# Turning the normed tokens in 32x32 blocks on VectorE and placing the blocks by transfers through DRAM, instead of transposing them on TensorE

## The chip, the cores and the metric

The kernel runs on one core of a Trainium2 chip. The metric is the device time of one execution in microseconds. The kernel was timed three times before the change; the median counts. TensorE (PE) multiplies matrices and transposes by a matmul with the identity, VectorE (DVE) and ScalarE (ACT) work on elements, GpSimd (POOL) does a little of the same, and SyncE (SP) issues nearly all transfers. Each engine works through its own instructions in order and waits on semaphores for the others.

## The reference

Four layers are chained on `x`, 8 sequences of 256 tokens of 512 features, all float32. Three of them contain a step "normalize every token, scale and shift its features by a vector that belongs to the sequence, multiply by weights"; it is this step that the change touches, five times over: the attention and the MLP of layer 0, the attention and the MLP of layer 1, and the attention of layer 2. Layer 3 (eight small experts with a norm) is not touched.

```python
# layer 0 (ada_rms, twice: ahead of the attention and of the MLP)
n = x * jax.lax.rsqrt(jnp.mean(jnp.square(x), axis=-1, keepdims=True) + EPS)
scale = t @ tw.T
return n * (w * (1.0 + scale))[:, None, :]
...
q = (h @ Wq.T).reshape(b, s, NQ, HD).transpose(0, 2, 1, 3)
scores = jnp.einsum('bkgsd,bktd->bkgst', qg, k) / jnp.sqrt(jnp.float32(HD))
attn = jax.nn.softmax(scores, axis=-1)
x = res + ctx @ Wo.T
...
mlp = jax.nn.silu(h @ Wg.T) * (h @ Wu.T) @ Wd.T
```

Layer 1 has a norm with mean and variance, 16 heads of 32 and a GELU MLP; layer 2 the same norm, 16 heads on 4 key heads, and a mask.

## The kernel before

A sequence is two tiles of 128 tokens by 512 features (tokens on the partitions). All products need the features on the partitions, so every normed sequence is transposed to `hT` (128 x 4 x 256: four chunks of 128 features by 256 tokens).

`normed` (L414) takes mean and variance by bn_stats and bn_aggr (L422, L423) on DVE, the power -1/2 on POOL (L430, L431), and writes the normed tile to a buffer `n` (L436 for layer 0's form, L438 for the other), once for each of the two tiles. `h` (L479) is a generator: it calls `normed`, pauses, and lets `feature_major` (L464) transpose chunk by chunk on TensorE (L471, eight 128x128 transposes for a sequence, into two PSUM banks `C`). Each chunk is evicted from PSUM with its scale and shift by `modulated` (L456): DVE for the first two chunks (L450 in layer 0, L460 in layers 1 and 2), ACT for the other two (L454, L462). `h` is called 40 times: 8 sequences in each of the five steps.

Work that isn't on the main line is a list of generators, `queue`. The main line calls `some(us)` (L196), which gives them a credit of microseconds of TensorE time; each `yield` says how much was used, and `yield None` ends a turn. `rest` (L210) drains the queue. On top of this a scheduler reorders the finished program on each engine, so that instructions can stand earlier than the code's order.

`attend` (L536) is the main line of the three attentions. A step handles one sequence b and one group g of four heads: `scored` (L569, TensorE into four PSUM banks `A`), `softmax` (L575: the row maxima on DVE, L583 or, with a bias, L591; the exponentials on ACT, L596; the reciprocal of the sums L602, its turn in 32x32 blocks L606, a store of 16 KB to DRAM L609, and loads that broadcast the rows over the partitions, L614: two of 128 KB in attention 0, one in attentions 1 and 2). One step later the group's probabilities are transposed (`turned`, L626, with evictions by `copy`, L448 on DVE and L452 on ACT), multiplied by the values (`weighted`, L641) and scaled by the broadcast inverses (`ctxT`, L653). Attention 0 has two groups per sequence, attentions 1 and 2 four. At g == 0 the queue is drained, and `project(b + 1)` is put into it: `h` of the next sequence, the products of its queries, keys and values (`product_steps`, L512), the rotary terms or norms (L530, L531, L1246 to L1258), and the transposes of queries and keys (L1019, L1234). The output projection with `wo` (L512) and the sum into `x` (L1075, L1210) follow when all groups are done. `work` holds the TensorE time that a sequence's share of the queue takes.

`mlp` (L777) walks over 64 steps: two halves hh of the inner features, 8 sequences, four steps p each. A step has the products of `begun` and `ended` (L793), sums on ACT and DVE (L811 to L814, L823), and the products of `lower` (L842). In the first half, at p == 0, the queue gets `following(b + 1)` (L869): `h` of the next sequence, the sums that `blocked` (L750) forms of its chunks, and their stores to DRAM (L755, L757), from which the second half loads them again (L763, L766). In the second half's last sequence the next attention's `project(0)` is in the queue.

SP issues the transfers of weights (L734, L745), the `spread` stores and loads, and those of `blocked`, in one queue. `hT` has two buffers.

Of the kernel before, what the change touches and what calls it, by code (L numbers as in the profile page):

```python
# [20 lines left out]
F32 = mybir.dt.float32  # L24
# [6 lines left out]
P = 128  # L31
B, S, D = 8, 256, 512
NT = B * S // P
TB = S // P
KC = D // P
# [133 lines left out]
class Program:  # L169
    def __init__(self, ctx, tc, d, out):  # L170
        self.ctx, self.tc, self.nc, self.d, self.out = ctx, tc, tc.nc, d, out
        self.n = 0
        self.queue, self.credit = [], 0.0

    def pool(self, name, psum=False):
        return self.ctx.enter_context(
# [19 lines left out]
    def some(self, us):  # L196


        self.credit += us
        while self.credit > 0 and self.queue:  # L200
            try:
                did = next(self.queue[0])
            except StopIteration:
                self.queue.pop(0)
                continue
            if did is not None:
                self.credit -= did
            elif us < 1e6:
                break

    def rest(self):
        self.some(1e9)
        self.credit = 0.0

# [2 lines left out]
    def setup(self):  # L217
        nc, d = self.nc, self.d
        self.const = self.pool("const")
        self.xp = self.pool("xp")  # L220
        self.wqkvp = self.pool("wqkvp")
        self.wop = self.pool("wop")
        self.wbigp = self.pool("wbigp")
        self.work = self.pool("work")
        self.psum = self.pool("psum", psum=True)

        def c(shape, tag, **kw):
            return self.t(shape, tag, pool=self.const, **kw)

        self.condT = c([P, KC, 32], "condT")  # L230
        nc.gpsimd.memset(self.condT, 0.0)
        nc.sync.dma_start(
            self.condT[:, :, :B], d["condT"].rearrange("(k p) b -> p k b", p=P)
        )
        self.x = [self.t([P, D], f"x{i}", pool=self.xp) for i in range(NT)]
        self.tw = self.columns("tw1T", 1)
        for i in range(TB):
            self.load_x(i)
        self.vec = c([P, N_VEC], "vec")
        nc.sync.dma_start(self.vec, d["vec"])  # L240
        self.pos = c([P, NT], "pos", dtype=I32)
        nc.sync.dma_start(self.pos, d["posT"])
        self.inv_freq = c([P, 32], "inv_freq")
        nc.sync.dma_start(self.inv_freq, d["inv_freq"].to_broadcast([P, 32]))

        self.ident = c([P, P], "ident")
        make_identity(nc, self.ident)
        self.neg_half = c([P, 32], "neg_half")
        nc.gpsimd.memset(self.neg_half, -0.5)
        self.inv = [c([P, 32], f"inv{i}") for i in range(2)]  # L250
        for t in self.inv:
            nc.gpsimd.memset(t, 0.0)
        self.spread = [
            self.tc.dram_tile([32, P], F32, name=f"spread{i}") for i in range(4)
        ]
        self.n_spread = 0
        self.half_pi = c([P, 1], "half_pi")
        nc.gpsimd.memset(self.half_pi, math.pi / 2)

        self.mod0 = c([P, 8, B], "mod0")  # L260
        self.mod1 = c([P, 16, B], "mod1")
        self.mod2 = c([P, 8, B], "mod2")
        self.mod3 = c([P, 8, B], "mod3")
        self.scondT = c([P, KC, 32], "scondT")
        nc.scalar.activation(self.scondT, self.condT, AF.Silu)
# [145 lines left out]

    def normed(self, xs, eps, rms=False):  # L414

        nc = self.nc
        n = len(xs)
        mv = self.t([P, n, 2], f"mv{n}", 2)
        r = self.t([P, n], f"r{n}", 2)
        for i, x in enumerate(xs):  # L420
            st = self.t([P, 6], "st", 3)
            nc.vector.bn_stats(st, x)  # L422
            nc.vector.bn_aggr(mv[:, i, :], st)  # L423
        mean, var = mv[:, :, 0], mv[:, :, 1]
        if rms:
            nc.vector.tensor_tensor(r, mean, mean, ALU.mult)
            nc.vector.tensor_tensor(r, r, var, ALU.add)
            nc.gpsimd.tensor_scalar(r, r, eps, None, ALU.add)
        else:
            nc.gpsimd.tensor_scalar(r, var, eps, None, ALU.add)  # L430
        nc.gpsimd.tensor_tensor(r, r, self.neg_half[:, 0:n], ALU.pow)  # L431
        rows = []
        for i, x in enumerate(xs):
            y = self.bank("n")
            if rms:
                nc.vector.tensor_scalar(y, x, r[:, i : i + 1], None, ALU.mult)  # L436
            else:
                nc.vector.tensor_scalar(  # L438
                    y, x, mv[:, i, 0:1], r[:, i : i + 1], ALU.subtract, ALU.mult
                )  # L440
            rows.append(y)
        return rows
# [33 lines left out]
            evacuate(c0, m.rearrange("p (c t) -> p c t", c=2))  # L476
            yield 0.87

    def h(self, b, eps, mod, scale_at, shift_at, rms=False, blocks=False):  # L479


        rows = self.normed([self.x[TB * b + t] for t in range(TB)], eps, rms)
        yield None
        hT = self.t([P, KC, S], "hT")

        def place(c):
            if not blocks:
# [1 line left out]
            at = 2 * (c // 2)  # L489
            return hT[:, at : at + 2, P * (c % 2) : P * (c % 2 + 1)]  # L490

        def evacuate(c0, m):
            for c in range(2):
                scale = mod[:, scale_at + c0 + c, b : b + 1]
                shift = None if shift_at is None else mod[:, shift_at + c0 + c, b : b + 1]
                in_ = m[:, c, :]
                if blocks:
                    in_ = in_.rearrange("p (t q) -> p t q", t=TB)
                self.modulated(c0 // 2, place(c0 + c), in_, scale, shift)

        yield from self.feature_major(rows, evacuate)
        yield None
        return hT

    def product(self, *args):
# [27 lines left out]

    def attend(self, n_groups, hd, project, value, finish, work, key_tiles=(2, 2), biased=None,  # L536
               extra=None, then=None, spare=None, inverse=None):

# [11 lines left out]
        nc = self.nc  # L552
# [3 lines left out]
        at = [0, wide[0]]  # L556
# [104 lines left out]
        for i in range(B * n_groups + 1):  # L661
# [19 lines left out]
                    turned(j, last[2][0][j])  # L681
            if ahead is not None:
                ahead = (b, g, softmax(ahead[2]))
            if last is None:
                self.some(3 * quantum)
            else:
# [79 lines left out]
            self.nc.sync.dma_start(t, kept[b, :, (4 + i) * S : (5 + i) * S])  # L766
        return hT, ts

    def mlp_input(self, *args, **kw):

        self.hT = yield from self.h(*args, **kw)

    def mlp_begin(self, name):
        self.kept = self.tc.dram_tile([B, P, 7 * S], F32, name=name)
# [252 lines left out]

    def project0(self, b, got):
        nc, w, cos, sin = self.nc, self.w0, self.cos, self.sin
        hT = yield from self.h(b, 1e-6, self.mod0, 0, None, rms=True)  # L1030
        qT = self.t([P, KC, S], "qT")
        kT, v = self.keys_values(b, ((S,), (TB, 64)))
        turn = []
# [43 lines left out]
    def layer0_attention(self):  # L1077
        self.ups = []

        def conditions(b):  # L1080
# [6 lines left out]
            else:  # L1087
# [4 lines left out]
                    self.layer0_up(i if i >= 0 else -1 - i, int(i >= 0))  # L1092

        self.attend(
            2, 64, self.project0, lambda v, g, j, k: v[:, k, :],
            lambda b, ctxT: self.added(b, ctxT, self.w0o), (10.5, 6.8),
            extra={
                0: (conditions(0), 7.7), 2: (conditions(2), 4.6),
                5: (self.sums_of_ups(0, 2), 0.0), 6: (self.sums_of_ups(2, 4), 0.0),
                7: (self.mlp_input(0, 1e-6, self.mod0, 4, None, rms=True, blocks=True), 1.74),  # L1100
            },
            then=lambda: self.mlp_begin("kept0"),
            spare=lambda: [self.ups[i][1][:, 7, :] for i in range(4)],
            inverse=[self.w0[:, k, 640:896] for k in range(4)],
        )

    def layer0_up(self, i, which):
# [8 lines left out]
    def layer0_mlp(self):  # L1116
# [52 lines left out]
        def finish(hh, b, ys):  # L1169
# [3 lines left out]

        self.mlp(
            ups, downs, down_sums, lambda i: self.layer0_up(4 + i, 1), load_next, act,
            lambda b: self.h(b, 1e-6, self.mod0, 4, None, rms=True, blocks=True), finish,
            (self.project1(0, self.got), 23.0),
        )


# [33 lines left out]
    def project1(self, b, got):  # L1214
# [2 lines left out]
        def heads(t):  # L1217
            return t.rearrange("p (h e) -> p h e", e=32)

        hT = yield from self.h(b, 1e-6, self.mod1, 0, 8)  # L1220

        def part(t, i):
            m = self.bank("C")
# [66 lines left out]
    def layer1_attention(self):  # L1290
# [32 lines left out]
        def value(v, g, j, k):  # L1323
            return v[:, k, (4 * g + j) * 32 : (4 * g + j + 1) * 32]

        self.attend(
            4, 32, self.project1, value, finish, (23.0, 6.8), biased=self.bias,
            extra={
                4: (self.sums_of_ups(0, 2), 0.0), 5: (self.sums_of_ups(2, 4), 0.0),
                7: (self.mlp_input(0, 1e-6, self.mod1, 4, 12, blocks=True), 1.74),  # L1330
            },
            then=lambda: self.mlp_begin("kept1"),
            spare=lambda: [self.ups[i][0][:, 7, :] for i in range(4)],
            inverse=[self.downs[i][2] for i in range(4)],
        )

    def layer1_up(self, i):
# [9 lines left out]
    def layer1_mlp(self):  # L1347
# [22 lines left out]
        def finish(hh, b, ys):  # L1370
# [8 lines left out]
        self.mlp(  # L1379
            self.ups, self.downs, lambda i: self.rights(*self.downs[i][0], *self.downs[i][1]),  # L1380
            lambda i: self.layer1_up(4 + i), lambda i: self.layer1_down(4 + i), act,
            lambda b: self.h(b, 1e-6, self.mod1, 4, 12, blocks=True), finish,
            (self.project2(0, self.got), 11.3),
        )


# [15 lines left out]

    def project2(self, b, got):
        nc, w = self.nc, self.w2
        hT = yield from self.h(b, 1e-5, self.mod2, 0, 4)
        qT = self.t([P, KC, S], "qT")
        kT, v = self.keys_values(b, ((S,), (TB, P)))
        m = self.bank("C")[:, :S]
# [32 lines left out]
    def layer2(self):  # L1441
        self.load_layer3()
        spare = self.t([P, 8, S], "wbig")
        self.attend(
            4, 32, self.project2, lambda v, g, j, k: v[:, k, j * 32 : (j + 1) * 32],
            lambda b, ctxT: self.added(b, ctxT, self.w2o), (11.3, 6.8), key_tiles=(1, 2),
            biased=self.mask, extra={7: (self.expert_inputs(0), 1.74)},
            spare=lambda: [spare[:, i, :] for i in range(4)],
            inverse=[spare[:, i, :] for i in range(4, 8)],
# [180 lines left out]
```

## Time and profile before

| | us |
|---|---|
| median of three timed runs | 2167.53 |
| lowest and highest | 2165.76, 2169.83 |
| profiled execution, its time | 2161.66 |
| its span, first to last instruction | 2159.9 |
| attention 0 with the setup | to about 280 |
| MLP 0 | 280 to 876 |
| attention 1 | 876 to 1310 |
| MLP 1 | 1310 to 1705 |
| attention 2 | 1705 to 2010 |
| experts (layer 3) | 2010 to 2159 |

The granted TensorE clock was 0.992 on average. The rows by line that concern the transposed tokens (line, engine, operation, tile, shape, count; then total busy time and mean ns of one; then idle time before and what ended it):

| line | engine | what | count | mean ns |
|---|---|---|---|---|
| L471 | PE | transpose of a 128x128 block of `n` | 320 | 290 |
| L436, L438 | DVE | normed tile, 128x512 | 32, 48 | 593, 644 |
| L450, L460 | DVE | chunk of `hT` from PSUM, 128x256 | 32, 48 | 475, 535 |
| L454, L462 | ACT | chunk of `hT` from PSUM, 128x256 | 32, 48 | 488, 557 |
| L606 | DVE | turn in 32x32 blocks, 128x32 | 80 | 206 |

Busy time of pipelined matmuls overlaps, so eight transposes cost less than eight times their mean. The transfers moved 106.71 MB in 93,425 packets, 49 GB/s over the span.

### The profile page before, as it was taken

The numbers are of one execution on the slowest core, as the hardware profiler recorded it, in microseconds if no ns is written. First come the engines' busy times: TensorE is split into PE (matmuls) and PEld (weight loads), VectorE is DVE, ScalarE is ACT, GpSimd is POOL, SyncE is SP. The second block draws the span as 40 slices with busy tenths as digits, with TensorE's granted clock in tenths as the row PEclk, the third lists the DMA queues.
The fourth block names the chain that finished last, engine by engine and source line by source line (L and its number), as shares of the span: only waits on it lengthen the run. The fifth ranks groups of instructions, "written<-read, shape, count | busy, mean of one in ns | idle before, by whom it ended". The sixth has DMA issues, their size and how long they took to land.

```text
span 2159.9 us, 36437 instructions
## 1 busy us (share of the span) xinstructions
PE 2089.9 (97%) x13522; PEld 1550.8 (72%) x13522; DVE 1335.2 (62%) x4444; ACT 757.2 (35%) x2330; POOL 293.5 (14%) x308
## 2 busy tenths in 40 slices
PE   7999999999999999999999999999999989999999
PEld 4555679999999999765555557999999855554444
DVE  6866665655666555665556566666666577676333
ACT  3423421111111111155555552222222255555644
POOL 2111100000000000334444341000000001010220
PEclk9999999999999999999999999999999999999999
DMA  8310230000320100210000022113211100000001
GB/s 303 115 56 21 69 124 18 30 24 18 90 78 21 33 18 18 69 44 19 17 20 17 12 63 68 45 62 93 93 48 45 49 20 18 18 19 20 6 35 44
DMA packets 93425, 106.71 MB, mean 49 GB/s; under 512 B 16512, under 2 KB 67392, under 8 KB 93248
## 3 DMA queue, kind: packets, MB, share of 16 engines
q1 hardware_dynamic: 93248, 104.38, 15.0%
q8 instruction: 107, 1.75, 0.3%
q14 instruction: 70, 0.57, 0.1%
HBM read 84.14 MB, written 20.22 MB: 48 GB/s over the span
## 4 chain that ended last, share of the span: by engine, by line
PE 86%; DVE 7%; DMA 3%; ACT 2%; POOL 1%; issue 1%; SPq 0%; ACTq 0%; DVEq 0%; POOLq 0%
PE C L793 28%; PE C L512 23%; PE A L842 18%; PE C L626 5%; PE A L569 4%; PE C L641 3%; DMA wqkv<-spread 1%; PE A L1499 1%; DVE p L591 1%; ACT p L596 1%; PE C L471 1%; PE C L1517 1%; DVE n L438 1%; DVE p L448 1%; DVE st L422 1%
## 5 line engine op out<-in xcount | busy, mean ns | idle before, releaser
L793 PE MATMUL C<-hT,wbig 128*128 128x128 f32 x3072 | 416.1, 275 | 2.6 <-DVE p L814 2.6
L793 PEld LDWEIGHTS C<-hT,wbig 128*128 128x128 f32 x3072 | 388.6, 192 | 11.8 <-issue 5.2
L793 PE MATMUL C<-ctxT,wbig 128*128 128x128 f32 x2304 | 319.8, 275 | 0.0
L512 PE MATMUL C<-wqkv,hT 128*128 128x512 f32 (+1 forms) x768 | 311.7, 545 | 4.0 <-DVE p L448 3.3
L596 ACT ACTIVATE p<-p,low 128x256 f32<-128x256 f32 (+1 forms) x512 | 241.1, 472 | 204.3 <-DVE low L591 202.9
L793 PEld LDWEIGHTS C<-ctxT,wbig 128*128 128x128 f32 x2304 | 288.0, 192 | 0.0
L842 PE MATMUL A<-wbig,p 128*128 128x256 f32 x1024 | 242.5, 379 | 0.0
L591 DVE CUSTOM_DVE_ANT_0 p<-A,row 128x256 f32<-128x256 f32 (+1 forms) x512 | 171.3, 386 | 90.3 <-PE C L641 65.9
L512 PEld LDWEIGHTS C<-wqkv,hT 128*128 128x128 f32 x768 | 129.9, 191 | 120.9 <-issue 110.8
L842 PEld LDWEIGHTS A<-wbig,p 128*128 128x128 f32 x1024 | 189.5, 190 | 23.1
L823 DVE TENSOR_TENSOR p<-p,C 128x256 f32<-128x256 f32 x192 | 79.1, 418 | 168.9 <-PE C L793 166.8
L811 ACT COPY p<-C 128x128 f32<-128x128 f32 x192 | 50.9, 265 | 376.8 <-PE C L793 376.8
L626 PEld LDWEIGHTS C<-ident,p 128*128 128x128 f32 x1152 | 130.6, 143 | 68.9 <-issue 40.7
L626 PE MATMUL C<-ident,p 128*128 128x128 f32 x1152 | 162.8, 282 | 9.7 <-ACT p L596 5.3
L512 PE MATMUL C<-wo,ctxT 128*128 128x512 f32 x336 | 158.4, 611 | 6.7 <-DVE ctxT L653 6.6
L430 POOL TENSOR_SCALAR r<-mv 128x2 f32<-128x2 f32 (+1 forms) x28 | 6.4, 230 | 865.7 <-DVE mv L423 865.2
L812 DVE TENSOR_TENSOR p<-p,C 128x128 f32<-128x128 f32 x192 | 54.5, 284 | 109.3 <-ACT p L811 107.4
L1156 ACT ACTIVATE p<-C 128x128 f32<-128x128 f32 x64 | 17.7, 277 | 285.4 <-DVE p L823 285.4
L512 PEld LDWEIGHTS C<-wo,ctxT 128*128 128x128 f32 x336 | 60.8, 193 | 79.2 <-issue 60.4
L448 DVE COPY p<-C 128x512 f32<-128x512 f32 (+1 forms) x160 | 100.6, 630 | 26.4 <-PE C L626 25.7
L596 ACT ACTIVATE p<-A,low 128x256 f32<-128x256 f32 x128 | 59.3, 477 | 120.5 <-DVE low L583 88.3
L452 ACT COPY p<-C 128x512 f32<-128x512 f32 (+1 forms) x160 | 85.1, 532 | 33.1 <-PE C L626 32.9
(214 smaller groups left out, 3054.4 us busy)
## 6 DMA issues: line engine op xcount, KB each, us to landing
kept<-hT SPq DMA_DIRECT2D x16, 512.0 KB
hT<-kept SPq DMA_DIRECT2D x16, 512.0 KB
wbig<-spread SPq DMA_DIRECT2D x64, 128.0 KB
wbig<-in_wada1T SPq DMA_DIRECT2D x6, 1024.0 KB
kept<-ctxT SPq DMA_DIRECT2D x48, 128.0 KB
ctxT<-kept SPq DMA_DIRECT2D x48, 128.0 KB
n<-gammas SPq DMA_DIRECT2D x24, 256.0 KB
x<-in_x SPq DMA_DIRECT2D x16, 256.0 KB
```

The lines of the kernel that those rows point to most:

```text
L448: self.nc.vector.tensor_copy(out, in_)
L452: self.nc.scalar.copy(out, in_)
L512: self.nc.tensor.matmul(out, lhsT(k), rhs(k), start=(k == 0), stop=(k == n - 1))
L569: nc.tensor.matmul(s[j][:, at[q] : at[q] + wide[q]], lhsT(q), rhs(wide[q]), start=True, stop=True,)
L591: nc.vector.tensor_tensor_reduce(p[:, cols], s[j][:, cols], biased[:, cols], -1.0, BIG, ALU.add, ALU.min, low[:, q : q + 1],)
L596: nc.scalar.activation(p[:, cols], src[:, cols], AF.Exp, bias=low[:, q : q + 1], scale=sign, accum_out=tot[:, j, q : q + 1],)
L626: nc.tensor.transpose(m[:, n * P : (n + 1) * P], p[:, at[q] + k * P : at[q] + (k + 1) * P], self.ident,)
L641: nc.tensor.matmul(o[i * hd : (i + 1) * hd, c * S + q0 * P : (c + 1) * S], value(got[b][1], g, j, k), pT[j][:, mine[0] * P : (mine[-1] + 1 ...
L793: nc.tensor.matmul(m[:, c : c + P], w[:, k * P : (k + 1) * P], b[:, k * P : (k + 1) * P], start=(first and k == 0), stop=(k == steps - 1), ...
L812: nc.vector.tensor_tensor(g[:, 0, :], g[:, 0, :], m[:, P : 2 * P], ALU.add)
L823: nc.vector.tensor_tensor(g[:, 1:3, :], g[:, 0, :].unsqueeze(1).to_broadcast([P, 2, P]), m[:, 2 * P : 4 * P].rearrange("p (i t) -> p i t", ...
L842: nc.tensor.matmul(acc[at][:, half * S : (half + 1) * S], left, right, start=(p == 0 and half == 0), stop=(p == 3), skip_group_check=True,)
```

## The change

`h` no longer transposes on TensorE, except in a form called `quick`. A new `prepare` computes the norm and writes the normed tiles straight into `hT`, with the features of a token regrouped so that a transposition of every 32x32 block (one DVE instruction on 128x1024) leaves blocks that are right inside and stand in the wrong places. Four stores write it to a DRAM tile `turn` (128 KB each, in pieces of 1 KB), and `fetch` loads it back into the same `hT` by eight transfers (64 KB each, in pieces of 128 bytes), each block to its place. Two of them bring one chunk. Scale and shift are then applied in place, SBUF to SBUF, by the same `modulated`: DVE for chunks 0 and 2, ACT for chunks 1 and 3 (before: 0 and 1, 2 and 3).

`prepare` is called two sequences ahead in the attentions (at g == 0 of sequence b for b + 2, or for the MLP's first sequence), `fetch` at a later group, and `h` waits until a few calls of `some` have passed (`at`), so that its place in the program is behind the landing. In the MLPs prepare, fetch and use come in one generator, in three successive steps. The quick form stays for sequences 0 and 1 of attention 0 and sequence 1 of attentions 1 and 2: 4 of the 40 calls. The yields of 0.87 us for the transposes go, and the credits of `work`, `extra` and the MLPs' tails are cut by that amount.

New lines shift the numbering of the changed kernel by up to 85. Its lines: the block turn L515, the stores L520, the fetches L536, the in-place modulation L462, L472 (DVE) and L466, L474 (ACT), TensorE's remaining transposes L483, the products L586, the transposes of p L702, the weighted sum L717.

```diff
-    def normed(self, xs, eps, rms=False):
+    def normed(self, xs, eps, rms=False, outs=None):
...
-            y = self.bank("n")
+            if outs is None:
+                y = self.bank("n")
+            else:
+                y, x = outs[i], x.rearrange("p (k c i) -> p c k i", k=KC, c=4)
...
+    def prepare(self, name, b, quick=False):
+        eps, _, _, _, rms, blocks = self.stage(name)
+        xs = [self.x[TB * b + t] for t in range(TB)]
+        hT = self.t([P, KC * S], "hT")
+        if quick:
+            self.ready[name, b] = [hT, self.normed(xs, eps, rms), None, 0]
+            return
+        nc = self.nc
+        y = hT.rearrange("p (c k t i) -> p c k t i", c=4, k=KC, t=TB)
+        self.normed(xs, eps, rms, [y[:, :, :, t, :] for t in range(TB)])
+        nc.vector.transpose(hT, hT)
+        kept = self.turns[self.n_turn % 3]
+        self.n_turn += 1
+        to = kept.rearrange("(c i) (a x) -> a i c x", c=4, a=4)
+        for a in range(4):
+            nc.sync.dma_start(
+                to[a], hT[32 * a : 32 * a + 32, :].rearrange("p (c x) -> p c x", c=4)
+            )
+        self.ready[name, b] = [hT, None, kept, 0]
+
+    def fetch(self, calls):
+        for (name, b), entry in self.ready.items():
+            hT, _, kept, _ = entry
+            if kept is None:
+                continue
+            parts = kept.rearrange("p (a k t j) -> p k t a j", a=4, k=KC, t=TB)
+            to = hT.rearrange("p (m n a j) -> p m n a j", m=4, n=2, a=4)
+            for k in range(KC):
+                for t in range(TB):
+                    m, n = (2 * (k // 2) + t, k % 2) if self.stage(name)[5] else (k, t)
+                    self.nc.sync.dma_start(to[:, m, n], parts[:, k, t])
+            entry[2:] = None, self.calls + calls
+
+    def h(self, name, b, quick=False):
+        if (name, b) not in self.ready:
+            self.prepare(name, b, quick)
+            yield None
+            self.fetch(1)
+        hT, rows, _, at = self.ready[name, b]
+        while self.calls < at:
+            yield None
...
+        if rows is None:
+            for c in range(KC):
+                placed(c, c, place(c))
...
             if ahead is not None:
                 ahead = (b, g, softmax(ahead[2]))
+                if g == 0:
+                    for c in (1, 2) if b == 0 else (b + 2,):
+                        if c < B:
+                            self.prepare(name, c, quick=c == 1)
+                        elif c == B and after is not None:
+                            self.prepare(after, 0)
+                else:
+                    self.fetch(3)
```

## The prediction

> **What bounds the kernel now.** I read the page's busy shares first, then the busy time of each engine by stage, then the chain of waits inside each kind of stage.
>
> ```profile
> PE 2089.9 (97%) x13522; PEld 1550.8 (72%) x13522; DVE 1335.2 (62%) x4444; ACT 757.2 (35%) x2330; POOL 293.5 (14%) x308
> ```
>
> TensorE is the bound on average, with VectorE at 62% behind it. The average hides the stages (microseconds, then busy time of PE, PEld, DVE, ACT, POOL, the clock, the DMA share and GB/s):
>
> ```profile
> 3.00:280.00 277.00, 254.83 (x1452) 152.36 (x1453) 190.49 (x567) 105.22 (x340) 42.57 (x73) 0.99 0.34 112
> 280.00:876.00 596.00, 592.46 (x4444) 562.85 (x4443) 363.41 (x1170) 93.63 (x285) 6.50 (x14) 0.99 0.13 43
> 876.00:1310.00 434.00, 421.41 (x2407) 236.72 (x2406) 261.09 (x891) 222.42 (x683) 173.87 (x124) 0.99 0.11 32
> 1310.00:1705.00 395.00, 391.85 (x2686) 367.19 (x2685) 260.50 (x804) 98.78 (x282) 12.77 (x20) 1.00 0.20 67
> 1705.00:2010.00 305.00, 283.74 (x1974) 167.73 (x1973) 207.55 (x918) 166.84 (x626) 36.84 (x46) 0.98 0.06 18
> ```
>
> Rows 2 and 4 are the two MLPs: TensorE idles 3.5 and 3.2 us in all, so every TensorE instruction there is on the path. Rows 1, 3 and 5 are the attentions: TensorE idles 22, 13 and 21 us. The chain in an MLP shows the price of the work that is removed:
>
> ```profile
> 343.51 3.02 PE A L842 x14
> 346.53 2.68 PE C L793 x24
> 349.21 0.87 PE C L471 x8
> 350.08 0.43 PE A L842 x2
> 350.52 3.57 PE C L793 x32
> ```
>
> The eight transposes of one h() (L471) cost 0.87 us, and the chain never leaves TensorE. In an attention the same eight lie elsewhere, between two sequences (TensorE in attention 2; the bracket is the idle time before and who ended it):
>
> ```profile
> 1871.24 0.87 PE L626 MATMUL C<-ident,p 128*128 128x128 f32 x6
> 1871.95 1.04 PE L471 MATMUL C<-ident,n 128*128 128x128 f32 x8
> 1873.81 0.63 PE L641 MATMUL C<-p,v 128*32 128x256 f32 x6 [0.82 <-DVE p L448]
> 1874.38 0.49 PE L569 MATMUL A<-kT,qT 32*128 32x128 f32 x4
> 1875.08 0.84 PE L641 MATMUL C<-p,v 128*32 128x256 f32 x10 [0.21 <-ACT p L452]
> ```
>
> After them TensorE waits 0.82 and 0.21 us for evicted probabilities. So removing the eight alone would only lengthen that wait; it pays if other products move into the gap. In attention 0 the chain leaves TensorE for a transfer at this place:
>
> ```profile
> 199.04 1.97 DMA spread<-invT
> ...
> 201.62 7.97 DMA wqkv<-spread
> ```
>
> That broadcast of the softmax inverses lands 8 us after its issue, and the weighted sum's scaling (L653) waits for it.
>
> **The change part by part.**
>
> *Removed from TensorE:* 36 of the 40 h() calls lose their eight transposes; the listing of the changed kernel's instructions by engine has 32 of them instead of 320. The 14 calls that run inside the two MLPs' steps (sequences 1 to 7 of each) are worth 14 x 0.87 = 12.2 us, if the block turn is ready in time.
>
> *Moved on TensorE:* in that listing the next sequence's projections (L512) now stand between the transposes of p (L626) and the weighted sum (L641): 12 matmuls in attention 0 (4.35 us by the 1.95 us of four 128x512 and half a us of four 128x128 in the timeline), 8 in attention 1 (3.6 us), 6 in attention 2 (some 2 us). They fill the gap: 1.0 us per sequence in attention 0, 0.93 in attention 1, 0.82 + 0.21 in attention 2.
>
> *Added on VectorE:* per sequence one block transpose of 128x1024. Before has only the 128x32 form (L606, 206 ns). A copy costs 276 ns for 128 columns and 682 for 512 (L448), 1.06 ns a column, so 206 + 992 x 1.06 = 1.25 us; I bound it by 1.0 (the 539 ns of 512 columns in L438 as the slope) and 2.5 us (twice). 36 of them make 45 us. The two hT evictions per sequence leave PSUM: 535 ns for 256 columns (L460) against 539 for 512 columns from SBUF (L438), so each saves some 0.2 us. In the MLPs VectorE works 25.8 of 38.0 us in a period, so this is covered. In the attentions it isn't wholly: the transpose stands ahead of a copy of p (L448). In attention 2 that copy ends 1.2 us later, at 1874.95; TensorE comes to it at 1871.95 + 2.6 = 1874.6, and loses 0.35. In attention 1 the projections cover it. In attention 0 both normalizing steps (0.5 us more) and the transpose precede the eviction of qT (L450, ends 199.6), which the scores (L569, 200.25) need: 1.05 us are lost.
>
> *Added on SP and the transfers:* per sequence 4 stores of 128 KB and 8 fetches of 64 KB, the latter in 128-byte pieces. An issue costs 0.37 to 0.56 us (L614, L734), a store-to-load round trip 1.97 us (above). Stores: 4 x 0.45 + 2 = 3.8 us. Fetch j lands 2 + (j - 1) x 0.45 us after that at best and with 0.9 us each (the spacing at which two 256 KB loads landed) at worst. Chunk 0 needs two fetches, chunk 3 all eight: 6.3 to 6.7 us and 9.0 to 12.1 us after the transpose. The extra traffic is 1 MB per sequence, 3.5 us at the 302 GB/s of a backed-up window, in stages whose DMA share is 0.06 to 0.34; I count nothing for it where no broadcast is under way. The landing of the chunks is what the changed kernel newly waits for, on VectorE for chunks 0 and 2, on ScalarE for 1 and 3, both in program order.
>
> *When it is needed:* in MLP 0 the listing puts the in-place modulation 10.6 us of work behind the transpose, in MLP 1 two steps (11 us). VectorE has 12 us of idle time in a period, and the matmuls that use hT start steps later: no loss. In attention 2 chunk 0 is wanted some 8 us and chunk 2 some 10 us after the transpose; the queue holds a spread store and load between stores and fetches, and the fetches come to 8.8 and 10.6: under 1 us late, and what stands behind (softmax of the next group) is wanted by TensorE 8 us later. In attention 1 chunk 3 comes 9 to 12 us after and delays ScalarE's copies of p (L452); TensorE has 5.6 us of output projection and 3 us of other work first. Its loss is 0 to 2.5 us; I take 1.2, nearer the fast issue of L614. In attention 0 the last store, or the fetches, stand behind two spread loads that take 8 us to land. If their packets queue, chunk 2 comes 5 us after VectorE wants it, ahead of the ctxT that the output projection needs; if not, nothing. That touches four of six sequences; I take 2.5 us each, the middle.
>
> The Trainium skill speaks against this kind of move: "DMA: Bandwidth & Descriptors", section Specifications, gives 512 B as the least transfer for the full rate and a read-modify-write below it. If 128-byte pieces cost what 512-byte ones do, the fetches run at a quarter of the 302 GB/s of the backed-up window at 142.5 us, 0.5 MB in 7 us; attention 1 and 2 would then lose 2.5 and 2 us a sequence, and the sum would be about zero instead of the one below. No row of before has 128-byte fetches to decide it.
>
> *The sum.* MLPs -12.2. Attention 2: 6 x (0.87 + 1.03 - 0.35) = -9.3. Attention 1: 6 x (0.87 + 0.93 - 1.2) = -3.6. Attention 0: 6 x (0.87 + 1.0 - 1.05) = -4.9, and 4 x 2.5 = +10. In all -20.0 us. The profiled execution took 2161.66 us (span 2159.9 and 1.8 around it), which makes 2141.7; the median of the three timed runs is 2167.53, 5.9 above it, so I forecast 2147.5 us.
> With every doubt for the change (no late fetch): -12.2 - 9.3 - 10.8 - 4.9 = -37. With each against it (2.5 us in attention 1, 2 us in attention 2, 5 us in attention 0's four): -12.2 + 2.7 + 4.2 + 15.1 = +10.
>
> **The rivals.**
>
> 1. *Late fetches (slower).* The place is ScalarE's and VectorE's in-order wait for the chunks in the attentions. If the fetches queue as the six loads of L734 did at 134.96 us (8.07 us, 1.35 each), eight need 10.8 us, and chunk 3 lands 16.6 us after the transpose, 7 later than counted. With some 3.5 us of cover it costs 3.7 us in each of 18 attention sequences, 66 us; against -37 that is +29: 2197 us. It decides from 37 / 18 = 2.1 us per sequence on. For it: many small pieces, and a queue that other loads share. Against it: those six loads moved 256 KB each, the fetches a quarter of that.
> 2. *Nothing lasting.* The MLPs gain 12 us and the attentions give it back through 1 us of wait per sequence beyond the terms above: about 2167 us. For it: VectorE carries half of the chain between sequences already. Against it: projections now stand there.
> 3. *The full gain.* Fetches always in time: 2167.5 - 37 = 2130.5 us. For it: DMA share 0.06 in attention 2. Against it: the 8 us broadcasts in attention 0.
>
> That the change doesn't do what it says has little room, since the listing shows the transposes gone.
>
> **How the numbers follow.** Forecast 2147.5 us (own range 2134 to 2162): 0.40. Full gain: 0.18. Nothing lasting: 0.11. Late fetches: 0.31. A measurement of this kernel can tell some 0.2%, 4.3 us, from no change. Faster is the first two less a little, 0.57; same 0.12; slower 0.31. The range goes from 2128, 2.5 us below the full gain, to 2188, which leaves out the worse half of the late fetches.
>
> **What would show it.** MLP steps without L471 and periods of 37.1 and 24.6 us instead of 37.97 and 25.47; a transpose of about 1.25 us; at most 1 us of TensorE idle time between sequences in attention 2; fetches landing within 12 us of the transpose. I am wrong if VectorE or ScalarE idle for microseconds before the in-place modulation and TensorE idles behind them, or if the MLPs show waits for hT.

## The result and the profile after

The changed kernel takes 2160.34 us (median of 6 runs, 2158.70 to 2162.43), the kernel before 2166.65 (median of 6, 2164.05 to 2169.83): a ratio of 0.9972, 95% interval 0.9959 to 0.9985. That is a gain of 6.3 us, where 20 were forecast. The whole profile hardly differs (the page of the changed kernel):

```profile
PE 2069.4 (96%) x13234; PEld 1525.0 (71%) x13234; DVE 1356.7 (63%) x4480; ACT 763.8 (35%) x2332; POOL 292.8 (14%) x308
```

TensorE is busy 20.5 us less than before, and its share falls to 96%: what was taken from it came back as waiting. To see where, the stages must be set side by side by the same pieces of work. The start of MLP 0 is the first of its matmuls with `hT`; the first line is from the group of that line in the kernel before, the second from the kernel after (shortest, median and longest ns, then first and last start in us):

```profile
L793 PE MATMUL C<-hT,wbig x2048: 272/275/340, 298.5 to 904.6; 128*128 128x128 f32 x187
```

```profile
L877 PE MATMUL C<-hT,wbig x2048: 272/275/335, 332.2 to 919.2; 128*128 128x128 f32 x187
```

MLP 0 begins 33.7 us later. The same reading of the other landmarks (last matmul of an MLP's second product, first of the next stage) gives the table; the two profiled executions have spans of 2159.9 and 2158.3 us, so its rows add up to 1.6 us and not to the 6.3 us between the medians (the profiled execution of the kernel before was some 5 us faster than its median).

| stage, us | before | after | measured | forecast |
|---|---|---|---|---|
| setup and attention 0 | 298.5 | 332.2 | +33.7 | +5.1 |
| MLP 0 | 623.1 | 617.2 | -5.9 | -6.1 |
| attention 1 | 388.7 | 376.3 | -12.4 | -3.6 |
| MLP 1 | 415.5 | 408.6 | -6.9 | -6.1 |
| attention 2 | 278.8 | 268.7 | -10.1 | -9.3 |
| experts | 155.4 | 155.3 | 0.0 | 0 |

Four stages gained 35 us, and the first one took 34 back. In the MLP the chain of waits of the changed kernel runs through products alone, without the 0.87 us of transposes; four steps of 9.28 us make the 37.1 us that the prediction gave for a period:

```profile
388.58 6.25 PE C L877 x56
394.84 3.02 PE A L926 x14
397.86 6.25 PE C L877 x56
```

In attention 2 TensorE's timeline has the next sequence's projections where the transposes and the two waits of 0.82 and 0.21 us were, and no bracket of idle time stands behind them:

```profile
1808.70 0.87 PE L702 MATMUL C<-ident,p 128*128 128x128 f32 x6
1809.41 1.89 PE L586 MATMUL C<-hT,wqkv 128*128 128x256 f32 x8
1811.14 1.88 PE L586 MATMUL C<-wqkv,hT 128*128 128x512 f32 x4
1812.95 0.86 PE L717 MATMUL C<-p,v 128*32 128x256 f32 x16
```

The block turn on VectorE costs what was worked out for it (group of the changed kernel; 1.25 us were forecast):

```profile
L515 DVE STREAM_TRANSPOSE hT<-hT 128x1024 f32<-128x1024 f32 x36 | 44.4, 1234 | 0.4
```

In attention 0 the chain of waits of the changed kernel tells what happens. The wait for the last store of a block turn stands on it five times between 122 and 269 us, 6.76 to 8.02 us long and 37.7 us in all; this is one of them (start, duration, what):

```profile
223.84 1.96 DMA spread<-invT
...
225.81 0.52 SPq L690
...
226.37 0.50 SPq L690
...
226.91 8.02 DMA turn<-hT
...
235.07 0.55 SPq L536
...
238.35 2.27 DMA hT<-turn
...
240.71 0.65 DVE hT L462
241.37 0.34 DVE ctxT L729
...
241.75 2.94 PE C L586 x4
```

The chain comes from the store of the softmax inverses, through the two broadcast loads that SP issues when that store has landed (L690), to the fourth store of the block turn, which SP issues behind them. This store lands 8.02 us after its issue. Only then do the fetches start (0.62 to 0.67 us apart), the last needed one lands 2.27 us after its issue, VectorE modulates, scales ctxT behind it in order, and TensorE, which waited for ctxT, goes on. SP's own timeline shows the same from the queue's side:

```profile
223.35 0.31 SPq L520 DMA_DIRECT2D turn<-hT  x1
223.84 0.56 SPq L685 DMA_DIRECT2D spread<-invT  x1
224.45 0.94 SPq L520 DMA_DIRECT2D turn<-hT  x2
225.81 1.06 SPq L690 DMA_DIRECT2D wqkv<-spread  x2
226.91 1.25 SPq L520 DMA_DIRECT2D turn<-hT  x1
235.07 5.26 SPq L536 DMA_DIRECT2D hT<-turn  x8
```

TensorE's own timeline shows that a wait costs more than its length. Four matmuls of the output projection take 1.98 us ahead of the wait for ctxT and the same four 2.94 us behind it:

```profile
237.77 1.98 PE L586 MATMUL C<-wo,ctxT 128*128 128x512 f32 x4
241.75 2.94 PE L586 MATMUL C<-wo,ctxT 128*128 128x512 f32 x4 [2.00 <-DVE ctxT L729]
```

The granted clock was 1.00 from 237.77 to 239.75 us and 0.65 from 241.75 to 244.69 us.

In the first 332 us ScalarE and VectorE wait 55.3 and 33.8 us for fetched blocks, up to 9.3 us at a time:

```profile
ACT hT L466 <- DMA hT<-turn: 55.3, 15, 9.3
```

```profile
DVE hT L462 <- DMA hT<-turn: 33.8, 11, 5.5
```

### The profile page after: what moved, and what is told of

The parts are those of the page before. It is cut to its first block, busy times and chain, and to the rows that moved or that the text cites. A ratio compares the mean times of both kernels' runs of the same rounds, so it can differ in the third digit from the quotient of the medians.

```text
span 2158.3 us, 36785 instructions
## 1 busy us (share of the span) xinstructions
PE 2069.4 (96%) x13234; PEld 1525.0 (71%) x13234; DVE 1356.7 (63%) x4480; ACT 763.8 (35%) x2332; POOL 292.8 (14%) x308
## 4 chain that ended last, share of the span: by engine, by line
PE 79%; DVE 7%; DMA 6%; SPq 3%; ACT 2%; POOL 2%; issue 1%; DVEq 0%; ACTq 0%; POOLq 0%
PE C L877 28%; PE C L586 18%; PE A L926 18%; PE C L702 4%; PE A L645 3%; PE C L717 3%; DMA turn<-hT 2%; SPq L536 2%; DVE p L667 1%; PE A L1586 1%; ACT p L672 1%; DMA hT<-turn 1%; DMA spread<-invT 1%; PE C L1604 1%; DMA wqkv<-spread 1%
## 5 line engine op out<-in xcount | busy, mean ns | idle before, releaser
L586 PE MATMUL C<-wqkv,hT 128*128 128x512 f32 (+1 forms) x768 | 314.4, 552 | 8.7 <-DVE hT L462 5.7
L586 PEld LDWEIGHTS C<-wqkv,hT 128*128 128x128 f32 x768 | 132.9, 194 | 132.4 <-issue 120.3
L702 PEld LDWEIGHTS C<-ident,p 128*128 128x128 f32 x1152 | 130.7, 144 | 84.7 <-issue 40.6
L702 PE MATMUL C<-ident,p 128*128 128x128 f32 x1152 | 166.9, 284 | 18.2 <-DVE p L460 9.0
L586 PE MATMUL C<-wo,ctxT 128*128 128x512 f32 x336 | 163.2, 617 | 11.6 <-DVE ctxT L729 11.6
L586 PEld LDWEIGHTS C<-wo,ctxT 128*128 128x128 f32 x336 | 59.6, 193 | 76.4 <-issue 54.3
L672 ACT ACTIVATION_READ_ACCUMULATOR p<-p,low 128x1 f32 x512 | 95.9, 187 | 0.0
```

The source lines that it names most:

```text
L586: self.nc.tensor.matmul(out, lhsT(k), rhs(k), start=(k == 0), stop=(k == n - 1))
L672: nc.scalar.activation(p[:, cols], src[:, cols], AF.Exp, bias=low[:, q : q + 1], scale=sign, accum_out=tot[:, j, q : q + 1],)
L702: nc.tensor.transpose(m[:, n * P : (n + 1) * P], p[:, at[q] + k * P : at[q] + (k + 1) * P], self.ident,)
```

## The experiments

The theory after this reading: the loss of attention 0 is the round trip of the blocks, held up behind the broadcast loads. The rivals were VectorE's added work on the chain between sequences, and something else in attention 0, such as the new order of the program or the clock (0.982 on average, 0.992 before). All times are medians of four runs beside runs of the kernel before on the same chip (2163.6 to 2164.1 us).

**a0_tensor: no block turn in attention 0.**

```diff
+                if name == "attention0":
+                    pass
-                if g == 0:
+                elif g == 0:
                     for c in (1, 2) if b == 0 else (b + 2,):
...
-        hT = yield from self.h("attention0", b, quick=b < 2)
+        hT = yield from self.h("attention0", b, quick=True)
...
-        self.hT = yield from self.h(name, 0)
+        self.hT = yield from self.h(name, 0, quick=name == "mlp0")
...
```

The credits of attention 0 go back to the 10.5 and 1.74 us of the kernel before.

> Attention 0 and the first sequence of MLP 0 are transposed on TensorE as before; everything else is the change. Theory (the loss of attention 0 is the round trip of the blocks, late behind the other transfers of SP's queue): MLP 0 begins at 298 us as before, not at 332, and all later gains stay (MLP 0 -6, attention 1 -12, MLP 1 -7, attention 2 -10): about 2127 us. Rival 1 (VectorE's added work): the same here. Rival 2 (something else in attention 0, a lower TensorE clock or the new order of the program): MLP 0 begins later than 315 us and the total stays above 2142.

2130.79 us, ratio 0.9849 (0.9835 to 0.9864); MLP 0 begins at 303.1 us. That is 4.6 us later than in the kernel before and than expected, and the total is 4 us above the expected 2127. The later stages keep their gains (MLPs 617.3 and 406.8, attentions 376.4 and 270.2). All but some 5 us of the loss sits in what the block turn does to attention 0; for more than that, "something else in attention 0" is out.

**a0_dve: VectorE's time alone.**

```diff
+            rows = self.normed(xs, eps, rms)
+            if name == "attention0":
+                for _ in range(2):
+                    self.nc.vector.transpose(rows[0], rows[0])
```

> As a0_tensor, and VectorE turns one of the two normed tiles of every sequence in attention 0 twice in its 32x32 blocks (twice is the tile itself): two instructions of 128x512, some 1.3 us, without any transfer. Theory: at most 1 us for each of 8 sequences, MLP 0 begins between 298 and 306 us. Rival 1 (the loss is VectorE's added time on the chain between sequences): MLP 0 begins at 318 us or later.

2122.80 us, ratio 0.9811 (0.9797 to 0.9826); MLP 0 begins at 296.5 us. No loss shows from the time that the turns take on VectorE. They stand here beside the norm of the next sequence, though, not two sequences ahead as in the change; what the earlier place costs is not in this run (w0_q3 below shows a case). That this kernel is 8 us faster than a0_tensor, with more work in it, was in nobody's expectation: the scheduler places other instructions otherwise too. Such a shift of some 7 us in attention 0 between two builds is what this comparison can't resolve, and its cause stays open.

**a0_late: TensorE for sequences 0 to 4.**

```diff
+                        if name == "attention0" and c < 5:
+                            continue
...
-        hT = yield from self.h("attention0", b, quick=b < 2)
+        hT = yield from self.h("attention0", b, quick=b < 5)
```

> The change, but sequences 0 to 4 of attention 0 are transposed on TensorE; 5 to 7 and the MLP's first go through DRAM. Theory: the first 20 us of the loss come from stores and fetches among the weight loads of the setup and go away, the 10 us of the last sequences (fourth store behind two spread loads, 8 us) stay: MLP 0 begins at 308 to 314 us, total 2137 to 2144. Rival 1: four of seven block turns stay, so four sevenths of 34 us: MLP 0 begins at 318 us.

2135.18 us, ratio 0.9868 (0.9852 to 0.9885); MLP 0 begins at 308.1 us. 24 us of the loss go with sequences 2 to 4, and some 10 stay with the rest. (The rest is five block turns, not four, and the change has eight: the trace has 20 and 32 stores ahead of MLP 0, since the turn of the MLP's second sequence is issued early too.) The number fits; the reason given for the first part (weight loads) has to be weighed against w0 and w0_q5 below.

**st_act: the stores issued from ScalarE.**

```diff
-            nc.sync.dma_start(
+            (nc.scalar if name == "attention0" else nc.sync).dma_start(
```

> The change, but in attention 0 ScalarE's queue issues the four stores instead of SP's. Theory in its strict form (a store waits because its packets stand behind the spread loads in the same queue): the stores land some 2 us after their issue, the fetches start 5 us earlier in the last sequences, MLP 0 begins at 312 to 322 us. If it is not the queue but the DMA engines themselves that are taken: stores still land 6 to 8 us after issue and MLP 0 begins at 330 us or later.

2142.49 us, ratio 0.9903 (0.9888 to 0.9918); MLP 0 begins at 316.2 us, within the strict form's range. But its own sign is only half there: after the last store's issue SP still waits 5.8 to 6.3 us in five of six cases before it can fetch, against 6.6 to 8.2 in seven of eight in the change. (The edit leaves the stores of the MLP's first two sequences with SP; there the wait is 8.1 and 6.7 us.) ScalarE's and SP's timelines of this kernel (two views):

```profile
186.89 0.31 ACTq L520 DMA_DIRECT2D turn<-hT  x1
```

```profile
183.94 1.09 SPq L690 DMA_DIRECT2D wqkv<-spread  x2
192.68 5.26 SPq L536 DMA_DIRECT2D hT<-turn  x8
```

The store is issued from another engine, 1.9 us after SP has issued the broadcasts, and the fetches still begin some 8 us after the second broadcast's issue, the time that such a broadcast takes. So a part of the wait is not SP's order but what the broadcasts occupy.

**wide: the broadcasts loaded row by row.**

```diff
-                nc.sync.dma_start(
-                    t, rows[c * per : (c + 1) * per, :].unsqueeze(1).to_broadcast([per, hd, S])
-                )
+                for i in range(per):
+                    r = c * per + i
+                    nc.sync.dma_start(
+                        t[i * hd : (i + 1) * hd, :], rows[r : r + 1, :].to_broadcast([hd, S])
+                    )
```

> The change, with one load per row of the softmax inverses (64 or 32 partitions each) in place of one load for two or four rows; the bytes are the same, SP issues two more loads per group in attention 0 and three more in attentions 1 and 2. Theory: a broadcast of two rows in one load keeps a few DMA engines busy for 8 us, and the fourth store waits for those. If a load of one row is spread over more engines, the broadcasts land in 3 to 4 us, the store in 3, and MLP 0 begins at 315 to 322 us (332 in the change). If the split does not change how a row is read, the broadcast lands after 8 us still and MLP 0 begins at 330 us or later. Attentions 1 and 2 stay within 2 us of the change (376 and 269 us).

2123.23 us, ratio 0.9812 (0.9796 to 0.9828); MLP 0 begins at 290.6 us, 42 us earlier than in the change and further than expected. The expectation of 2 us for attentions 1 and 2 failed both ways: attention 1 takes 372.9 us (3.4 less than in the change), attention 2 274.4 us (5.7 more), and MLP 1 411.5 (408.6 in the change). Row by row loads are not free there; whether it is SP's added issues that cost is not shown.

**a0_tensor_wide: both.** The two edits above together.

> As a0_tensor, with the broadcasts loaded row by row as in wide. Theory: with 11% of attention 0's chain in those broadcasts (some 32 us, 4 of 8 us each to be saved where TensorE has nothing else), MLP 0 begins at 285 to 297 us (303 in a0_tensor) and the total is 2113 to 2125 us. If TensorE's idle time there is hidden by other waits: 2129 to 2133 us.

2123.70 us, ratio 0.9818 (0.9803 to 0.9832); MLP 0 begins at 290.1 us, the same as in wide. With the broadcasts out of the way, the block turn in attention 0 costs nothing against TensorE's transposes that two builds can show.

**ahead_tensor: transposes on TensorE, two sequences ahead, in attentions 1 and 2.**

```diff
+        if name in ("attention1", "attention2") and b > 0:
...
+            for _ in self.feature_major(self.normed(xs, eps, rms), evacuate):
+                pass
+            self.ready[name, b] = [hT, (), None, 0]
+            return
```

> The change, but in attentions 1 and 2 the sequences from 1 on are transposed by TensorE, still two sequences ahead and evicted with scale and shift at once: no block turn, no transfers there. Theory (most of the gain of the attentions comes from the projections that can stand in TensorE's gap, because hT is ready early): attention 1 takes 381 to 384 us and attention 2 274 to 276 (change 376.3 and 268.7, before 388.7 and 278.8), since only 6 or 7 times 0.87 us come back. Rival (the gain is the removed transposes and the freed banks alone): 386 us or more and 277 or more.

2181.38 us, ratio 1.0082 (1.0067 to 1.0097): attention 1 takes 387.3 us and attention 2 283.7. The theory of this run fell, the rival's numbers came. TensorE's timeline shows why it is no clean test of early readiness:

```profile
1148.22 1.09 PE L483 MATMUL C<-ident,n 128*128 128x128 f32 x8
1149.15 1.04 PE L719 MATMUL C<-ident,p 128*128 128x128 f32 x8
1150.12 0.69 PE L662 MATMUL A<-kT,qT 32*128 32x256 f32 x2
1151.52 1.52 PE L603 MATMUL C<-wqkv,hT 128*128 128x512 f32 x3 [0.71 <-DVE hT L472]
```

The transposes are back in the gap between two sequences, and the projections behind them wait 0.71 us for an eviction of `hT` on VectorE. Writing the preparation earlier in the code doesn't give the filled gap by itself; how much of the 12.4 us of attention 1 each of the two, fewer matmuls and the gap, would bring alone stays open.

**before_w0 and w0: row by row loads in attention 0 only, without and with the change.** The edit of wide, for the case of two rows per load, in the kernel before and in the changed one.

> The kernel before, with attention 0's broadcasts of the softmax inverses loaded row by row (attentions 1 and 2 as they were). Theory: before the change the 8 us broadcast was on the chain too, so attention 0 shortens by 8 to 16 us and the total is 2148 to 2156 us; the change, put on top of it (w0), is then worth 30 us or more, against 6 without it. Rival (row by row loading is a gain of its own of 30 us and more, whatever the turn does): 2135 us or less, and the change on top is worth under 15 us.

2153.75 us, ratio 0.9946 (0.9929 to 0.9964); MLP 0 begins at 289.3 us, the other stages are as before. At the end of attention 0 the load of one row lands 2.63 us after its issue (chain of waits of this kernel); in the kernel before, the load of two rows at the same place took 8.34 us.

```profile
282.53 2.63 DMA wqkv<-spread
```

> The change, with row by row loads in attention 0 only. Theory: MLP 0 begins at 290 us as in wide, attention 2 comes back to 268 to 270 us (274 in wide, where SP issued three more loads per group), total 2115 to 2121 us.

2115.70 us, ratio 0.9770 (0.9752 to 0.9787); MLP 0 begins at 287.0 us, attention 2 takes 268.0. Both theories' numbers held: on this footing the change is worth 2153.75 - 2115.70 = 38 us, six times what it is worth with the old broadcasts. SP's timeline of w0:

```profile
202.51 1.23 SPq L693 DMA_DIRECT2D wqkv<-spread  x2
203.79 0.58 SPq L520 DMA_DIRECT2D turn<-hT  x1
206.31 1.23 SPq L536 DMA_DIRECT2D hT<-turn  x2
```

The order in the queue is the old one (store, broadcasts, fourth store, fetches), but the fetches begin 2.5 us after the fourth store, not 8.2. In the whole stage SP waits 46.2 us for these stores in the change and 11.5 us in w0 (total, times, longest):

```profile
SPq L536 <- DMA turn<-hT: 46.2, 10, 7.2
```

```profile
SPq L536 <- DMA turn<-hT: 11.5, 10, 1.9
```

TensorE executes 1450 matmuls up to MLP 0 both in the change and in w0 (first the change; columns as in the prediction's table of stages):

```profile
0.00:332.16 332.16, 275.12 (x1450) 159.33 (x1451) 205.00 (x595) 112.03 (x348) 45.12 (x84) 0.91 0.45 128
```

```profile
0.00:286.96 286.96, 257.03 (x1450) 152.13 (x1451) 204.52 (x594) 112.04 (x348) 45.51 (x84) 0.97 0.50 143
```

Of the 45.2 us between them, 27.1 are idle time of TensorE (57.0 against 29.9). The other 18.1 us are matmuls taking longer, at a mean granted clock of 0.91 against 0.97.

**w0_q3 and w0_q5: w0, with sequence 2, or 2 to 4, of attention 0 on TensorE as well.** The edits are those of a0_late with 3 or 5, on w0.

> As w0, with sequence 2 of attention 0 transposed on TensorE too, so that no block turn falls into the setup's first 65 us. Theory (the rest of the loss is stores and fetches among the setup's loads): TensorE is busy 34 us or more of the first 50 (28 in wide), MLP 0 begins at 280 to 287 us, total 2106 to 2115 us.

> As w0, with sequences 0 to 4 of attention 0 on TensorE. Theory: no store or fetch meets the weight loads any more, MLP 0 begins at 280 to 290 us; whether it beats w0_q3 depends on 2 x 0.87 us more of transposes against fetches behind loads. Total 2107 to 2118 us.

2110.63 us, ratio 0.9747 (0.9729 to 0.9765), and 2110.24 us, ratio 0.9744 (0.9729 to 0.9758); MLP 0 begins at 280.6 and 284.1 us. These beat both kernels, by 50 and 54 us. In the first 50 us of w0, and then of w0_q3 (stage, then busy time of PE, PEld, DVE, ACT, POOL, clock, DMA share, GB/s):

```profile
0.00:50.00 50.00, 27.24 (x132) 17.48 (x133) 31.42 (x115) 19.41 (x50) 7.53 (x23) 0.86 0.85 301
```

```profile
0.00:50.00 50.00, 34.65 (x160) 21.87 (x161) 30.99 (x118) 19.89 (x51) 7.21 (x22) 0.93 0.94 328
```

Without the first block turn TensorE is 7.4 us busier there, and MLP 0 begins 6.4 us earlier. Both expectations came true in their numbers, but not for their reason: in w0 SP issues its first store at 50.08 us, so no store and no fetch runs in these 50 us. What TensorE waits for is VectorE (first TensorE's timeline of w0, then VectorE's of w0 and of w0_q3):

```profile
49.04 10.66 PE L586 MATMUL C<-wqkv,hT 128*128 128x512 f32 x32 [5.74 <-DVE hT L462]
```

```profile
48.42 0.48 DVE L462 TENSOR_SCALAR hT<-C,mod 128x256 f32<-128x256 f32 x1
```

```profile
38.63 0.88 DVE L462 TENSOR_SCALAR hT<-C,mod 128x256 f32<-128x256 f32 x2 [0.95 <-PE C L483]
```

In w0 the scaling of sequence 1's chunks, on which TensorE's projections wait, stands on VectorE behind the norm work that `prepare` brings forward (from 43.95 to 48.4 us). In w0_q3, where sequences 1 and 2 are not prepared ahead, it comes 9.8 us earlier. The change has the same wait (5.73 us). So this part of the loss is VectorE's work in an earlier place. What stores and fetches among the setup's loads cost is not isolated by any run; between w0 and w0_q5 the whole block turn of sequences 2 to 4 is worth 2.9 us, not 20, and w0_q5, with two turns fewer than w0_q3, begins MLP 0 3.5 us later, which is within the 7 us that two builds differ by.

## Why the prediction was off

*Three of the four gains were sized well.* MLPs: 12.8 us measured, 12.2 forecast. Attention 2: 10.1 against 9.3. Attention 1 gained 12.4 where I had 3.6: its 1.2 us for late fetches per sequence were too many, and 0.87 + 0.93 us per sequence alone make 10.8. The block turn took 1.234 us against 1.25. The rival "late fetches" counted 3.7 us in each of 18 attention sequences. In attention 1 the longest waits for fetched blocks are 2.9 us on ScalarE and 2.4 us on VectorE, in attention 2 2.7 and 2.0 us, and no wait of TensorE for `hT` is listed in either. In attention 0 its sign did come (waits of up to 9.3 us ahead of the in-place modulation, TensorE idle behind them), but through a late store, not through fetches that queue. "Nothing lasting" was near the measured time with another place: it is attention 0 alone that gives the gains back. The full gain of 37 us, worked out as a rival, is near the 38 us that w0 shows over before_w0. The sum fits better than its parts: attention 0, counted with 4.9 us, has 2.3 there.

*The step that failed* is the term of attention 0: "If their packets queue, chunk 2 comes 5 us after VectorE wants it ... That touches four of six sequences; I take 2.5 us each, the middle." The mechanism was right and the size was not: +10 in the sum, with 20 as the upper bound, and some 36 measured. Row by row loads shorten attention 0 by 332.2 - 287.0 = 45.2 us with the change and by 298.5 - 289.3 = 9.2 without it, so 36 us hang on the change and the two-row broadcasts together; by the pair wide and a0_tensor_wide they are 332.2 - 290.6 = 41.6 and 303.1 - 290.1 = 13.0, which leaves 29. Four things were wrong in the term. It meets every block turn of the stage, eight with the MLP's first two sequences, not four of six: the time from the last store's issue to the first fetch is 6.6 to 14.4 us in all eight of the change, and 2.4 to 3.9 in w0. The price is the wait of the store *and* the fetches that start behind it, since the fetches' 5.3 us of issue no longer lie beside anything. A wait of TensorE was counted at its length, and the matmuls behind it ran longer too: 27 of the 45 us between the change and w0 are idle time and 18 are matmuls at a lower granted clock. And the middle of an open range was taken, although the trace of before showed that the broadcast took 8 us in a stretch whose DMA share was 0.11 (202.0 to 209.5 us), which left open what else it holds up.

The price is not the same for every turn. Of the 36 us, 21 belong to sequences 2 to 4 (24.1 us between the change and a0_late, less the 2.9 between w0 and w0_q5), 7 us a turn, and 15 to the other five turns, 3 us each, close to the 2.5 that I took. As differences of four builds these are rough. The term on VectorE in attention 0 (1.05 us a sequence) also left out the start of the stage, where the norm brought forward makes TensorE wait 5.73 us.

That the total of 2160.3 us lies between the 2128 and 2188 us that were given is luck: attention 0 came out 28.6 us worse than its terms, attention 1 8.8 us better, and the two partly cancel.

*How a broadcast is read.* The Trainium skill, "DMA: Bandwidth & Descriptors", section Rules for kernel authors, says that the slowest dimension of an access pattern larger than one sets how many engines work, so that a leading dimension of two confines a whole transfer to at most two engines. The runs agree with it: the DMA share of 0.11 during the two-row load is a little under two of 16 engines, that load lands after 8 us, and a load of one row over 64 partitions, half the bytes, after 2.6 us. No view here names the engines of a transfer. I had not weighed this rule, and had weighed the 512 bytes that the same page's section Specifications gives as the least transfer for the full rate. The quarter rate that I had drawn from it didn't come: away from the setup's loads eight fetches, 0.5 MB, were issued in 5.26 us, 100 GB/s and not 75, and the last one on the chain landed 2.3 to 2.5 us after its issue. Whether the short pieces cost something less than that is not shown.

*The clock* of 0.982 in the change goes with these waits: it is 0.992 in the profiled execution of w0, with the same block turns.

## What to carry to other kernels

A transfer that has a broadcast or a small outer dimension should be looked at for how long it lands before anything new is put on the same path: here its own consumer lost 9 us to it in the whole stage before the change, and a round trip beside it some 30 more. When a change moves a step to a round trip through DRAM, cost the queue order of each stage in which it runs, and not only the free round trip. Count the idle time of TensorE and the clock behind it separately. And compare stages, not totals: a gain of a few microseconds was 35 won and 34 lost, and the lost part could be had back by an edit elsewhere.

## What had not been expected of the hardware

The same 128 KB, in two loads of one row each instead of one load of two rows, take SP 1.2 us to issue instead of 0.5, and most of the wait is gone: the fourth store's round trip falls from some 8 us to 2.5. Issuing the stores from another engine's queue (st_act) only brought it to about 6. After a wait of 2.00 us four matmuls took 2.94 us instead of 1.98, at a granted clock of 0.65 instead of 1.00. Fetches in pieces of 128 bytes went at the pace of their issue, 0.66 us for each 64 KB, and landed 2.3 to 2.5 us after it.
